# Attention with a gated feed-forward: the order of the first group and the places of the weight signs

## The chip, the cores and the metric

The kernel runs on one core of a Trainium2 chip. The metric is the device time of one execution in microseconds (us), as the median of five runs. The engines of a core are called here as the profile calls them: PE is TensorE (matrix products), PEld its weight load, DVE is VectorE, ACT is ScalarE, POOL is GpSimd and SP is SyncE, which here issues nearly all DMAs. L300 is line 300 of the kernel before; in the kernel after the change the same code stands 4 to 11 lines lower.

## The reference

The input x has 4 sequences of 512 positions and 1024 channels, in fp32.

```python
xn = layernorm(x)                                    # no scale, no shift
q, k, v = xn @ Wq, xn @ Wk, xn @ Wv                  # 16 heads of 64
q, k = rotary(q), rotary(k)
p = softmax(where(causal, q @ k.T, -1e9) / 8)        # per head, 512 x 512
s = (p @ v) @ Wo

r = softmax(xn @ gate_w.T)                           # router over 8 experts
g = silu((xn * (r @ in_scale)) @ sign(weight).T * (r @ out_scale) + bias)

out = x + s * g
```

## The kernel before

**Work.** Let b be one of the 4 sequences and g one of 4 groups of four heads. The kernel goes through 16 groups k = 0 to 15, in the order of (b, g). In each it projects the group's q, k and v (`project`, three matrices m = 0, 1, 2, so that one matrix is a key (b, g, m)), and on the way does the attention of group k − 1. After the last group come the rest of the feed-forward (`gated`, `ffn`) and the output projection (`project_out`), which the change does not touch.

**Start.** x arrives in four tiles of 128 rows. Each is normalised: two bn_stats of 512 columns, an aggregate (mean and variance), the root on ACT (`std`, L185), reciprocal and subtract-multiply on DVE (L193). PE then transposes it in eight 128 x 128 blocks (`transpose_x`, L205), four to a PSUM bank `xtp`, and ACT copies each bank into X (L211). X holds one sequence, channels by rows.

**Projection.** `project` multiplies a key's weights with X by a scheme of seven half-size products in place of eight. It needs four sums of weight quarters, S1 to S4 (`form_w`, DVE, L249), for every key, and four sums of X quarters, T1 to T4 (`form_x`, DVE, L261), once for a sequence. The order of the products before is: a11·b11 and a12·b21, which need neither S nor T; S3·T3; S2·T2; S1·T1; a22·T4; S4·b22. A product is four matmuls in the program and eight on the chip (fp32 takes two passes). While a key is worked on, DVE forms the S sums of the next. The results are put together by p1 and p5 copies on ACT (L333, L354), additions on DVE (L327, L356) and one on POOL (the part add, L355). The sums are called c for q and k and v for v. q and k then go through `rotary`: eight swaps on ACT for a pair of tiles (L269, L270), one operation on DVE (L271, `rot`), two on POOL (L272, L273).

**Attention.** `attention_pieces` lists the pieces for group k − 1: five transposes of probabilities (`ptp`, L457, copied to `pT`) for each of two pending units, `scores_1`, `scores_3` and `scores_02` with `values` between. A score block is: matmuls (L391), mask and row maximum on DVE (L402, L406), exponentials on ACT (L409), reciprocal on DVE (L417), scaling on POOL (L419). The probabilities from `scores_02` (p0) are transposed at the beginning of the next group.

**Extras.** In the groups with g = 0 (k = 0, 4, 8, 12) further pieces are put between these: `load_sign` and `make_sign` take two of the eight tiles of `weight` and make their signs (four DVE operations to a tile, L573 and L574), and `router` works in three steps: `lg` (64 matmuls, L495), its transpose `lt` with the softmax, and the transpose `rt` of the result. At k = 0 there are also `load_scales` (32 small DMAs on SP) and `split_scales`, once for in_scale and once for out_scale (isc, osc): one cast on ACT (L561) and three DVE operations over 128 x 1024 (L562 to L564).

**Order.** PE's instructions run in the order in which the program is written (a manual schedule). `interleave` writes them: after each piece come so many matmuls of the projection that 84 of them spread evenly over the pieces. DVE, ACT, POOL and SP get their order from a scheduler of the framework, except in a block at the start in which DVE and ACT follow the program too. The extras' places come from one rule:

```python
step = max(1, (len(pieces) + len(extra)) // (len(extra) + 1))
for n, e in enumerate(extra):
    pieces.insert(min(len(pieces), (n + 1) * step + n), e)
```

For k = 4, 8 and 12 this puts the six extras at places 3, 7, 11, 15, 19 and 21 of 0 to 21, in the order loads, router, sign, router, sign, router.

**Buffers.** All products, transposes and router results share a ring of four PSUM banks (`bank`); the scores have banks of their own. Three weight tiles of 1 MB are held. Later x tiles, the staged `weight` tiles and the scales share two buffers (`xip`). Every S and T sum has one buffer.

Of the kernel before, what the change touches and what calls it, by code (L numbers as in the profile page):

```python
# [22 lines left out]
NE = 8  # L23
# [28 lines left out]
def attn_gated_ffn_kernel(  # L52
# [111 lines left out]
    def load_x(b, t):  # L164
        if b == 0:
            xt = X1[:, t, :]
        else:
            xt = xip.tile([P, E], F32, tag="x", name=f"x_{b}_{t}")
        nc.sync.dma_start(out=xt, in_=x[(b * TPB + t) * P : (b * TPB + t + 1) * P, :])
        xin[b, t] = xt  # L170

    MV = {}

    def statistics(b, t):
        xt = xin[b, t]
        stats = st.tile([P, 2, 6], F32, tag="bn", name=f"bn_{b}_{t}")
        for j in range(2):

            tc.keep_in_program_order(
                nc.vector.bn_stats(stats[:, j, :], xt[:, j * HALF : (j + 1) * HALF])  # L180
            )
        mv = st.tile([P, 2], F32, tag="mv", name=f"mv_{b}_{t}")
        nc.vector.bn_aggr(mv, stats)
        std = st.tile([P, 1], F32, tag="std", name=f"std_{b}_{t}")
        nc.scalar.activation(std, mv[:, 1:2], AF.Sqrt, bias=eps)  # L185
        MV[b, t] = mv, std

# [5 lines left out]
        nc.vector.tensor_scalar(xt, xt, mv[:, 0:1], rstd, op0=ALU.subtract, op1=ALU.mult)  # L193

    def layernorm(b, t):
        statistics(b, t)
        normalize(b, t)

    def transpose_x(b, t, g):
        if b not in X:  # L200
            X[b] = xp.tile([P, NC, S], F32, tag="X", name=f"X_{b}")
        tp = tp_bank(f"xtp_{b}_{t}_{g}")
        for j in range(4):
            c = 4 * g + j
            nc.tensor.transpose(tp[:, j, :], xin[b, t][:, c * P : (c + 1) * P], ident)  # L205
        dst = X[b][:, 4 * g : 4 * g + 4, t * P : (t + 1) * P]

        if g == 0 and b > 0:
            nc.vector.tensor_copy(dst, tp)
        else:  # L210
            nc.scalar.copy(dst, tp)  # L211
        if g == 1:
            nc.sync.dma_start(
                out=xn_d[b, t].rearrange("p (c q) -> p c q", c=NC),
                in_=X[b][:, :, t * P : (t + 1) * P],
            )
# [62 lines left out]
    def project(b, g):  # L279

        for m in range(3):
# [15 lines left out]
            def product(ps, wq, xq):  # L297
                if m < 2:
                    for k in range(4):
                        nc.tensor.matmul(  # L300
                            ps, lhsT=wq[:, k, :], rhs=xq[:, k, :], start=(k == 0), stop=(k == 3)
                        )
                        yield
                else:

                    for j in range(2):
                        for k in range(4):
                            nc.tensor.matmul(  # L308
                                ps[:, j * P : (j + 1) * P],
                                lhsT=xq[:, k, j * P : (j + 1) * P],  # L310
                                rhs=wq[:, k, :],
                                start=(k == 0),
                                stop=(k == 3),
                            )
                            if k % 2:
                                yield

            def halves(n):

                ps = bank(f"pj_{un}_{n}")  # L320
                return ps, ps[:, :TH], ps[:, TH:]
# [14 lines left out]
                rotary(*turn.pop(0))  # L336
            _, p, r = halves(2)
            yield from product(r, SF[key, 3], TF[b, 3])
            yield from product(p, SF[key, 2], TF[b, 2])
            u2, u3 = part(2), part(3)  # L340
            add(u2, p, p1)
# [2 lines left out]
                rotary(*turn.pop(0))  # L344
            if after:
                form_w(after, 3)
            ps, p, r = halves(3)
            yield from product(r, SF[key, 1], TF[b, 1])
            if after:
                form_w(after, 1)  # L350
                form_w(after, 2)
# [300 lines left out]
            nc.scalar.copy(Z[q, i][:, k * HALF : (k + 1) * HALF], ps[n])  # L652


    for t in range(TPB):
        load_x(0, t)
    for m in range(3):
        load_w(0, 0, m)
    nc.sync.dma_start(out=cos_sb, in_=cos)
    nc.sync.dma_start(out=sin_sb, in_=sin)  # L660
    nc.sync.dma_start(out=gw[:, :, :NE], in_=gate_wT.rearrange("(c p) e -> p c e", p=P))

    first = project(0, 0)
    with tc.manual_schedule(engines={DVE, ACT}):
        statistics(0, 0)
        for t in range(TPB):
            if t + 1 < TPB:
                statistics(0, t + 1)
            if t == 2:
                next(first)  # L670
            normalize(0, t)
            for g in range(2):
                transpose_x(0, t, g)
            for _ in range((0, 3, 3, 0)[t]):
                next(first)
        for n in (3, 1, 2):
            form_w(keys[0], n)
        next(first)
        for n in (3, 1, 2, 4):
            form_x(0, n)  # L680
        form_w(keys[0], 4)

    def attention_pieces(k, late):
# [41 lines left out]
    for k, (b, g) in enumerate(groups):  # L725
        pieces = []
        if k > 0:
            pieces, late = attention_pieces(k - 1, late)
        extra = []
        if g == 0:  # L730
            extra = [
                lambda: (load_sign(2 * b), load_sign(2 * b + 1)),
                lambda: router(b, 0),
                lambda: make_sign(2 * b),
                lambda: router(b, 1),
                lambda: make_sign(2 * b + 1),
                lambda: router(b, 2),
            ]
            if b == 0:
                extra[5:5] = [lambda: (load_scales(in_scale), load_scales(out_scale))]  # L740
                extra += [lambda: split_scales(isc), lambda: split_scales(osc)]
        elif g == 1 and b + 1 < B:
            for t in range(2):
                load_x(b + 1, t)
        elif g > 1 and b + 1 < B:
            t0 = 2 * (g - 2)
            for t in range(t0, t0 + 2):
                layernorm(b + 1, t)
            extra = [
                lambda t=t, h=h: transpose_x(b + 1, t, h) for t in range(t0, t0 + 2) for h in range(2)  # L750
            ]
            if g == 2:
                extra.append(lambda: [load_x(b + 1, t) for t in (2, 3)])
# [4 lines that stand above are left out]
        if b == B - 1:  # L758

            if g < 2:  # L760
                load_xn(g)
            if g in (1, 2):
                pieces.insert(3, lambda: in_scales(g - 1, score_banks))
            if g == 3:
                z_place[0] = [xip.tile([P, E], F32, tag="x", name=f"z0_{i}") for i in range(2)]
                pieces.insert(3, lambda: out_scales(0, score_banks))
        fill = project(b, g) if k else first
        interleave(pieces, fill, 3 * 7 * 4)
        if g == NGRP - 1 and b + 1 < B:
            for n in (3, 1, 2, 4):  # L770
                form_x(b + 1, n)
# [297 lines left out]
```

## Time and profile before

| | |
|---|---|
| five runs | 1203.81, 1201.61, 1203.27, 1201.52, 1203.18 us |
| median | 1203.18 us |
| profiled execution | 1203.81 us, of which the span is 1202.1 us |
| mean granted TensorE clock | 0.995 |
| PE busy | 1172.8 us, 98% of the span |
| DVE busy | 774.6 us, 64% |
| ACT busy | 493.1 us, 41% |
| POOL busy | 536.3 us, 45% |
| DMA | 122.04 MB, 102 GB/s over the span |

The span runs from the first to the last instruction that the profiler recorded; the device time is 1.7 us longer. A timeline row gives start, busy time, engine, line, operation, tiles and shapes, and how many instructions it stands for; in brackets is the idle time of the engine before it, and what ended it. In a list of waits the three numbers are the sum in us, the number of waits and the longest.

### The profile page before, as it was taken

How to read it: one execution, taken by the hardware profiler on the slowest of the kernel's cores; microseconds unless marked ns; L12 is line 12 of the kernel's file. 1: busy time of each engine (PE TensorE's matmuls, PEld its weight loads, DVE VectorE, ACT ScalarE, POOL GpSimd, SP SyncE). 2: the span in 40 equal slices, each digit the busy share in tenths (PEclk: the TensorE clock that was granted, in tenths of full speed). 3: DMA queues.
4: the chain of work that ended last, by engine and by line, in shares of the span. 5: the costliest groups of instructions: out<-in, count | busy, mean ns of one | idle time of the engine just before them, and what ended most of it. 6: DMA issues, size and time to landing. Idle time of an engine off the chain costs nothing.

```text
span 1202.1 us, 17805 instructions
## 1 busy us (share of the span) xinstructions
PE 1172.8 (98%) x6696; PEld 890.5 (74%) x6696; DVE 774.6 (64%) x1395; ACT 493.1 (41%) x1134; POOL 536.3 (45%) x596
## 2 busy tenths in 40 slices
PE   6999999999999999999999999999999999999997
PEld 5988888878878887887888878887764456645663
DVE  6878676786767678576767866666864533453342
ACT  2453655344464644355464534446432121222120
POOL 0464536353443635243353534255355445544543
PEclk9999999999999999999999999999999999999999
DMA  8423423322143232223335122210503623432320
GB/s 298 127 70 119 135 80 95 117 86 93 44 126 112 80 118 94 64 80 114 105 98 184 52 74 80 76 52 18 202 14 135 194 81 106 145 109 71 106 70 35
DMA packets 59814, 122.04 MB, mean 102 GB/s; under 512 B 5200, under 2 KB 40528, under 8 KB 53584
## 3 DMA queue, kind: packets, MB, share of 16 engines
q1 hardware_dynamic: 55008, 111.98, 28.8%
q0 software_dynamic: 4720, 8.92, 2.1%
q8 instruction: 53, 0.87, 0.3%
q14 instruction: 33, 0.27, 0.1%
HBM read 95.45 MB, written 25.43 MB: 101 GB/s over the span
## 4 chain that ended last, share of the span: by engine, by line
PE 90%; DVE 7%; ACT 2%; issue 1%; POOL 0%; DMA 0%; ACTq 0%; DVEq 0%
PE pj L300 32%; PE wo L933 16%; PE pj L308 13%; PE ff L821 9%; PE pv L473 6%; PE sc L391 6%; PE ptp L457 6%; DVE nmx L406 2%; ACT p L409 1%; PE xtp L205 1%; DVE sc L402 1%; PE lg L495 1%; DVE rot L271 1%; DVE S L249 0%; DVE lo L633 0%
## 5 line engine op out<-in xcount | busy, mean ns | idle before, releaser
L419 POOL TENSOR_SCALAR p<-p,rs 128x128 f32<-128x128 f32 (+3 forms) x256 | 169.3, 673 | 204.6 <-DVE rs L417 204.6
L409 ACT ACTIVATE p<-sc,nmx 128x128 f32<-128x128 f32 (+3 forms) x256 | 132.7, 524 | 154.2 <-DVE nmx L406 145.8
L300 PE MATMUL pj<-T,S 128*128 128x256 f32 x768 | 182.3, 380 | 2.2 <-DVE T L261 2.2
L300 PEld LDWEIGHTS pj<-T,S 128*128 128x128 f32 x768 | 140.1, 190 | 20.6 <-DVE T L261 3.0
L300 PE MATMUL pj<-X,w 128*128 128x256 f32 x512 | 127.3, 391 | 6.4 <-DVE v L356 6.4
L355 POOL TENSOR_TENSOR part<-part,part 128x256 f32<-128x256 f32 x48 | 37.6, 783 | 200.4 <-ACT part L354 196.4
L272 POOL TENSOR_TENSOR sw<-sw,sin_sb 128x512 f32<-128x512 f32 x64 | 84.0, 1313 | 85.2 <-ACT sw L270 81.8
L300 PEld LDWEIGHTS pj<-X,w 128*128 128x128 f32 x512 | 95.5, 196 | 19.6 <-DVE v L356 7.1
L406 DVE TENSOR_REDUCE nmx<-sc 128x2 f32<-128x512 f32 (+3 forms) x128 | 103.6, 819 | 2.5
L249 DVE TENSOR_TENSOR S<-w 128x512 f32<-128x512 f32 x96 | 82.4, 860 | 32.8 <-PE pj L300 28.5
L821 PE MATMUL ff<-sg,hi 128*128 128x512 f32 x256 | 103.5, 404 | 0.0
L463 ACT COPY pT<-ptp 128x512 f32<-128x512 f32 x96 | 56.1, 587 | 115.2 <-PE ptp L457 114.3
L821 PE MATMUL ff<-sg,lo 128*128 128x512 f32 x256 | 99.9, 390 | 0.0
L457 PE MATMUL ptp<-ident,p 128*128 128x128 f32 x640 | 95.6, 273 | 2.9 <-DVE z_t L831 1.1
L308 PE MATMUL pj<-S,T 128*128 128x128 f32 x768 | 93.8, 280 | 2.3 <-DVE S L249 2.3
L308 PEld LDWEIGHTS pj<-S,T 128*128 128x128 f32 x768 | 89.7, 195 | 4.2 <-DVE S L249 2.5
L457 PEld LDWEIGHTS ptp<-ident,p 128*128 128x128 f32 x640 | 78.9, 141 | 18.5 <-DVE z_t L831 1.6
L269 ACT ACTIVATE sw<-c 32x512 f32<-32x512 f32 x128 | 80.4, 628 | 27.6 <-DVE c L327 25.7
L273 POOL TENSOR_TENSOR rot<-rot,sw 128x512 f32<-128x512 f32 x64 | 84.6, 1322 | 4.8
L391 PE MATMUL sc<-rot,rot 64*128 64x384 f32 (+3 forms) x512 | 82.0, 449 | 0.0
L270 ACT ACTIVATE sw<-c 32x512 f32<-32x512 f32 x128 | 80.4, 628 | 1.8
L473 PE MATMUL pv<-pT,v 128*64 128x256 f32 (+3 forms) x512 | 76.0, 439 | 0.0
(137 smaller groups left out, 1991.6 us busy)
## 6 DMA issues: line engine op xcount, KB each, us to landing
w<-in_wqkv SPq DMA_DIRECT2D x48, 1024.0 KB
x<-in_x SPq DMA_DIRECT2D x16, 512.0 KB
xn_d<-X SPq DMA_DIRECT2D x16, 512.0 KB
at_d<-at SPq DMA_DIRECT2D x32, 256.0 KB
xp<-xn_d SPq DMA_DIRECT2D x16, 512.0 KB
ap<-at_d SPq DMA_DIRECT2D x16, 512.0 KB
xr<-in_x SPq DMA_DIRECT2D x16, 512.0 KB
wb<-in_wb SPq DMA_DIRECT2D x8, 512.0 KB
```

What stands on the lines that cost most here:

```text
L272: nc.gpsimd.tensor_tensor(sw, sw, sin_sb, op=ALU.mult)
L273: nc.gpsimd.tensor_tensor(rot, rot, sw, op=ALU.add)
L300: nc.tensor.matmul(ps, lhsT=wq[:, k, :], rhs=xq[:, k, :], start=(k == 0), stop=(k == 3))
L308: nc.tensor.matmul(ps[:, j * P : (j + 1) * P], lhsT=xq[:, k, j * P : (j + 1) * P], rhs=wq[:, k, :], start=(k == 0), stop=(k == 3),)
L391: nc.tensor.matmul(ps[:, h, :], lhsT=Q[u][r : r + D, i * P : (i + 1) * P], rhs=K[u][r : r + D, : (i + 1) * P], start=True, stop=True,)
L406: nc.vector.tensor_reduce(nmx, ps, AX.X, ALU.max, negate=True)
L409: nc.scalar.activation(pt[:, h, :], ps[:, h, :], AF.Exp, bias=nmx[:, h : h + 1], accum_out=ssum[:, h : h + 1],)
L419: nc.gpsimd.tensor_scalar(pt[:, h, :], pt[:, h, :], rs[:, h : h + 1], 1.0, op0=ALU.mult, op1=ALU.mult,)
L457: nc.tensor.transpose(tp[:, k, :], probs(u, i)[:, h, j * P : (j + 1) * P], ident)
L473: nc.tensor.matmul(pv[r : r + D, j * P :], lhsT=V[u][:, j, r : r + D], rhs=PT[u][:, n, o : o + (TPB - j) * P], start=(j == 0), stop=(j == ...
L821: nc.tensor.matmul(acc, lhsT=part[q][:, i, c, :], rhs=sg[4 * k + c // 2][:, (c % 2) * HALF : (c % 2 + 1) * HALF], start=(c == 0 and part i ...
L933: nc.tensor.matmul(ps, lhsT=lhs[:, k, :], rhs=rhs[:, k, :], start=(k == 0), stop=(k == 3))
```

## The change

The change has five parts.

1. Before the input arrives PE does 26 transposes of the identity into a spare bank, whose results nobody reads.
2. The DMAs at the start are issued in another order: x tiles 0 and 1, the first half (512 KB) of the first key's weights, x tiles 2 and 3, the second half, the router's weights, then the other two keys' weights and the rotary tables.
3. In the block at the start the statistics of tile t + 1 are split: its first half stands ahead of the normalisation of tile t, its second half, the aggregate and the root behind the transposes and copies of tile t. The last copy of tile 3 goes to DVE. T and S sums are formed in the order T3, S1, T1, T2, S2, T4, S4. S3 is formed ahead of the normalisation of tile 3. In the very first key the product S1·T1 comes ahead of S2·T2.
4. For k = 0 the extras stand in a written list: router step 0 first, loads, router step 1, both signs, the scales' loads, router step 2, both splits, and two empty pieces.
5. For k = 4, 8 and 12 the extras stand at written places 0, 5, 8, 9, 12 and 15, in the order loads, sign, router, sign, router, router. With that `scores_02` moves from place 17 to 19.

In the order that results, PE's instructions differ from before only in the first two groups and in groups 4, 8 and 12. On the scheduled engines the following moves too: in group 1, DVE has the three osc operations of `split_scales` ahead of the four S sums of key (0, 1, 1), where before they stood ahead of those of (0, 1, 2); ACT has the osc cast behind the eight rotary swaps of (0, 1, 0); POOL has the part add of (0, 1, 0) behind the scaling of both p3 tiles; SP issues the weights of key (0, 1, 1) behind the 32 small DMAs of the scales.

```diff
--- before.py
+++ after.py
@@ -169,16 +169,18 @@
         nc.sync.dma_start(out=xt, in_=x[(b * TPB + t) * P : (b * TPB + t + 1) * P, :])
         xin[b, t] = xt
 
-    MV = {}
-
-    def statistics(b, t):
-        xt = xin[b, t]
-        stats = st.tile([P, 2, 6], F32, tag="bn", name=f"bn_{b}_{t}")
-        for j in range(2):
-
-            tc.keep_in_program_order(
-                nc.vector.bn_stats(stats[:, j, :], xt[:, j * HALF : (j + 1) * HALF])
-            )
+    BN, MV = {}, {}
+
+    def half_statistics(b, t, j):
+        if j == 0:
+            BN[b, t] = st.tile([P, 2, 6], F32, tag="bn", name=f"bn_{b}_{t}")
+
+        tc.keep_in_program_order(
+            nc.vector.bn_stats(BN[b, t][:, j, :], xin[b, t][:, j * HALF : (j + 1) * HALF])
+        )
+
+    def deviation(b, t):
+        stats = BN[b, t]
         mv = st.tile([P, 2], F32, tag="mv", name=f"mv_{b}_{t}")
         nc.vector.bn_aggr(mv, stats)
         std = st.tile([P, 1], F32, tag="std", name=f"std_{b}_{t}")
@@ -193,7 +195,9 @@
         nc.vector.tensor_scalar(xt, xt, mv[:, 0:1], rstd, op0=ALU.subtract, op1=ALU.mult)
 
     def layernorm(b, t):
-        statistics(b, t)
+        half_statistics(b, t, 0)
+        half_statistics(b, t, 1)
+        deviation(b, t)
         normalize(b, t)
 
     def transpose_x(b, t, g):
@@ -205,7 +209,7 @@
             nc.tensor.transpose(tp[:, j, :], xin[b, t][:, c * P : (c + 1) * P], ident)
         dst = X[b][:, 4 * g : 4 * g + 4, t * P : (t + 1) * P]
 
-        if g == 0 and b > 0:
+        if (g == 0 and b > 0) or (g == 1 and (b, t) == (0, TPB - 1)):
             nc.vector.tensor_copy(dst, tp)
         else:
             nc.scalar.copy(dst, tp)
@@ -336,6 +340,10 @@
                 rotary(*turn.pop(0))
             _, p, r = halves(2)
             yield from product(r, SF[key, 3], TF[b, 3])
+            if pos == 0:
+
+                bank3 = halves(3)
+                yield from product(bank3[2], SF[key, 1], TF[b, 1])
             yield from product(p, SF[key, 2], TF[b, 2])
             u2, u3 = part(2), part(3)
             add(u2, p, p1)
@@ -344,8 +352,11 @@
                 rotary(*turn.pop(0))
             if after:
                 form_w(after, 3)
-            ps, p, r = halves(3)
-            yield from product(r, SF[key, 1], TF[b, 1])
+            if pos:
+                ps, p, r = halves(3)
+                yield from product(r, SF[key, 1], TF[b, 1])
+            else:
+                ps, p, r = bank3
             if after:
                 form_w(after, 1)
                 form_w(after, 2)
@@ -652,32 +663,55 @@
             nc.scalar.copy(Z[q, i][:, k * HALF : (k + 1) * HALF], ps[n])
 
 
-    for t in range(TPB):
-        load_x(0, t)
-    for m in range(3):
+
+    idle = bank("idle")[:, :P]
+    for _ in range(26):
+        nc.tensor.transpose(idle, ident, ident)
+    load_x(0, 0)
+    load_x(0, 1)
+
+    W[0, 0, 0] = wp.tile([P, 2, NC, P], F32, tag="w", name="w_0_0_0")
+
+    def load_half_w(i):
+        nc.sync.dma_start(
+            out=W[0, 0, 0][:, i].rearrange("p c n -> p (c n)"), in_=wqkv[0, 0][:, i * E : (i + 1) * E]
+        )
+
+    load_half_w(0)
+    load_x(0, 2)
+    load_x(0, 3)
+    load_half_w(1)
+    nc.sync.dma_start(out=gw[:, :, :NE], in_=gate_wT.rearrange("(c p) e -> p c e", p=P))
+    for m in (1, 2):
         load_w(0, 0, m)
     nc.sync.dma_start(out=cos_sb, in_=cos)
     nc.sync.dma_start(out=sin_sb, in_=sin)
-    nc.sync.dma_start(out=gw[:, :, :NE], in_=gate_wT.rearrange("(c p) e -> p c e", p=P))
 
     first = project(0, 0)
     with tc.manual_schedule(engines={DVE, ACT}):
-        statistics(0, 0)
+        half_statistics(0, 0, 0)
+        half_statistics(0, 0, 1)
+        deviation(0, 0)
         for t in range(TPB):
             if t + 1 < TPB:
-                statistics(0, t + 1)
-            if t == 2:
-                next(first)
+                half_statistics(0, t + 1, 0)
+            else:
+                form_w(keys[0], 3)
             normalize(0, t)
             for g in range(2):
                 transpose_x(0, t, g)
-            for _ in range((0, 3, 3, 0)[t]):
+            if t + 1 < TPB:
+                half_statistics(0, t + 1, 1)
+                deviation(0, t + 1)
+            for _ in range((0, 5, 2, 0)[t]):
                 next(first)
-        for n in (3, 1, 2):
-            form_w(keys[0], n)
         next(first)
-        for n in (3, 1, 2, 4):
-            form_x(0, n)
+        form_x(0, 3)
+        form_w(keys[0], 1)
+        form_x(0, 1)
+        form_x(0, 2)
+        form_w(keys[0], 2)
+        form_x(0, 4)
         form_w(keys[0], 4)
 
     def attention_pieces(k, late):
@@ -728,17 +762,33 @@
             pieces, late = attention_pieces(k - 1, late)
         extra = []
         if g == 0:
-            extra = [
-                lambda: (load_sign(2 * b), load_sign(2 * b + 1)),
-                lambda: router(b, 0),
-                lambda: make_sign(2 * b),
-                lambda: router(b, 1),
-                lambda: make_sign(2 * b + 1),
-                lambda: router(b, 2),
-            ]
-            if b == 0:
-                extra[5:5] = [lambda: (load_scales(in_scale), load_scales(out_scale))]
-                extra += [lambda: split_scales(isc), lambda: split_scales(osc)]
+            loads = lambda: (load_sign(2 * b), load_sign(2 * b + 1))
+            signs = [lambda n=n: make_sign(2 * b + n) for n in range(2)]
+            routing = [lambda n=n: router(b, n) for n in range(3)]
+            if k == 0:
+                pieces = [
+                    routing[0],
+                    loads,
+                    routing[1],
+                    *signs,
+                    lambda: (load_scales(in_scale), load_scales(out_scale)),
+                    routing[2],
+                    lambda: split_scales(isc),
+                    lambda: split_scales(osc),
+                    lambda: None,
+                    lambda: None,
+                ]
+            else:
+
+                for at, piece in (
+                    (0, loads),
+                    (5, signs[0]),
+                    (8, routing[0]),
+                    (9, signs[1]),
+                    (12, routing[1]),
+                    (15, routing[2]),
+                ):
+                    pieces.insert(at, piece)
         elif g == 1 and b + 1 < B:
             for t in range(2):
                 load_x(b + 1, t)
```

## The prediction, made before the changed kernel ran

> **What bounds the kernel now.** I read the page first (busy shares, the chain that ended last), then what TensorE waited for, then the timeline around each wait.
>
> ```profile
> PE 1172.8 (98%) x6696; PEld 890.5 (74%) x6696; DVE 774.6 (64%) x1395; ACT 493.1 (41%) x1134; POOL 536.3 (45%) x596
> PE 90%; DVE 7%; ACT 2%; issue 1%; POOL 0%; DMA 0%; ACTq 0%; DVEq 0%
> ```
>
> TensorE (PE) is the bound: busy 98%, 90% of the chain. Only its idle time and its slow time can be won; no matmul of the network is removed. Where it idled:
>
> ```profile
> PE xtp L205 <- DVE x L193: 9.0, 2, 8.8
> PE pj L300 <- DVE v L356: 6.4, 3, 2.2
> PE pj L308 <- DVE S L249: 2.3, 1, 2.3
> PE pj L300 <- DVE T L261: 2.2, 2, 1.6
> ```
>
> So: 8.8 us before the first transpose, three waits of 2.19, 2.195 and 2.03 us (6.42 together) where groups 5, 9 and 13 begin, one of 2.35 us at 93 us, and 1.55 + 0.61 us for the T forms at the start. The change touches the code around every one.
>
> Idle time costs twice. After the wait at 93.09 us the 128-column matmuls start 0.213 us apart instead of 0.112, until 96.8:
>
> ```profile
> 93.10:96.80 3.70, 3.70 (x18) 3.70 (x19) 3.67 (x4) 2.25 (x4) 3.70 (x7) 0.54 0.92 312
> ```
>
> (columns: window, length, busy PE, PEld, DVE, ACT, POOL, then the granted clock, 0.54.) The same happens for 3.41 us after the waits at 479 and 694 us, not after the one at 265.9. All slow stretches end and begin on one grid of 3.41 us; a window that was 31 to 40% busy was followed by a slow one, a window 46% busy was not (the 265.9 wait is split over two). A slow window loses half: 1.71 us. At the start the cadence is the slow one until 14.89; the window 8.06–11.47, 71% busy, did not end it, the next, fully busy, did.
>
> **The change, part 1: the start.** Before:
>
> ```profile
> 8.76 1.94 PE L205 MATMUL xtp<-ident,x 128*128 128x128 f32 x8 [8.76 <-DVE x L193]
> ...
> 11.21 0.30 ACT L185 ACTIVATE std<-mv,eps 128x1 f32<-128x1 f32 x1
> 12.13 0.59 ACT L211 COPY X<-xtp 128x512 f32<-128x512 f32 x1 [0.61 <-PE xtp L205]
> ...
> 20.82 1.99 PE L300 MATMUL pj<-T,S 128*128 128x256 f32 x8 [1.55 <-DVE T L261]
> ```
>
> The 26 idle transposes run from about 1.5 us (ident is written at 1.48); 26 x 0.213 (the slow cadence of L205) = 5.5 us, to 7.1. They lie in the 8.76 us in which PE had nothing, and cost nothing. Tile 0 is normalised 0.79 us earlier (half of tile 1's statistics, 0.64, and the 0.21 aggregate now stand behind it): ends 7.81. From 7.1 until the first product PE has only the first transposes, so a clock raised by the dummies would meet a window under 40% busy and fall again. I take it as slow there.
>
> What the reader must see in the ACT rows is the order: std of tile 2 (11.21) ran ahead of the copies of tile 1 (12.13). In the changed order std of tile t+1 stands behind both copies of tile t, so the tiles form a chain: norm end, +0.15, transposes and two copies 2.56 at slow clock, std 0.29, reciprocal and norm 1.05 = 4.05 us. Tile 1 ends at 11.9 (before 10.92). Five quarter products (10 matmuls) now stand in PE between the transposes of tiles 1 and 2, so tile 2's transposes wait for them: they start at 16.4 if the clock rises at 14.9, at 17.9 if at 18.3. X is complete at 21.3 or 23.0; I take R = 22.0 (before 18.43 + 1.07 = 19.5), 20.3 if PE were fast throughout. The last copy on VectorE in parallel saves 0.5 and is in this. After X: before, 13.0 us to the end of the first key (32.51), made of the T3 wait, five products of 1.73, the 0.61 wait, the router's lg of 1.95 and its transpose. After, lg stands where PE waited for T3: 1.95 + 5 x 1.73 + 0.11 = 10.7. End 32.7, **+0.2 us** (−1.5 with R = 20.3, +1.2 with 23.0). The loads move past each other on SP's queue, but x3 landed by 9.1 and the first w by 11.6 against norms at 16 and 20: hidden. Signs of tiles 0 and 1 now fall into the second key: 2.1 us each, beside about 8 us of other DVE work in its 12.1 us of PE: hidden.
>
> The skill's page "TensorE: Matmul & The Clock Gate", Part 4, says that PE-mode transposes do not count as busy for the clock gate, which speaks against the dummies altogether: by that rule R = 20.3 is out, and the sum stays as I have it. The rows leave it open, since the window of transposes that left the clock slow was only 71% busy; by them R = 20.3 can happen, and the sum would be 1.7 lower.
>
> **Part 2: a new wait in key (0,1,1).** Before, and the wait that it replaces:
>
> ```profile
> 86.39 1.06 ACT L561 CAST osc<-scales 128x1024 fp32r<-128x1024 f32 x1
> ...
> 91.13 1.30 DVE L564 SCALAR_TENSOR_TENSOR osc<-osc,is_high,scales 128x1024 fp32r<-128x1024 f32 x1
> ...
> 92.35 1.37 DVE L249 TENSOR_TENSOR S<-w 128x512 f32<-128x512 f32 x2
> 93.09 4.05 PEld L308 LDWEIGHTS pj<-S,T 128*128 128x128 f32 x21 [2.54 <-DVE S L249]
> 93.09 4.13 PE L308 MATMUL pj<-S,T 128*128 128x128 f32 x20 [2.35 <-DVE S L249]
> ```
>
> split_scales(osc) stood in DVE's queue ahead of the S forms of (0,1,2), and PE waited 2.35. In the changed order it is a key earlier: DVE has the two rot0 operations, then L562 to L564 for osc, then all four S forms of (0,1,1); and ACT has the osc cast behind the eight rotary swaps of (0,1,0). On SP, w of (0,1,1) is issued behind the 32 small scale loads; it still lands some 20 us ahead of use. On the clock of before: PE ends (0,1,0) at 72.79 and has two products without S, until 76.24. POOL's part add (L355), which c and so the swaps wait for, now stands behind the scaling of p3: p3 73.0 to 74.33, add to 75.07, c 75.1 to 75.5. Eight swaps x 0.64 end at 80.7; cast 1.05, 81.75; L562, L563, L564 to 84.95; S3 0.65, 85.6. PE loses 85.66 − 76.24 = **9.4 us** (8.2 if the part add could run ahead of p3 and c came at 73.9; 10.3 with the longest POOL rows, 1.13 for the add and 1.2 for a scaling). Such a gap fills two windows, so one to two slow windows follow: 1.7 to 3.4, I take 2.25. The old wait and its slow window go: 2.35 + 1.71 = 4.06. Sum 9.4 + 2.25 − 4.06 = **+7.6**.
>
> **Part 3: signs of groups 4, 8 and 12.** What made the 2.19 us:
>
> ```profile
> 262.89 0.71 DVE L573 TENSOR_SCALAR sg<-wb 128x512 fp32r<-128x512 f32 x1
> ...
> 263.53 0.41 DVE L406 TENSOR_REDUCE nmx<-sc 128x2 f32<-128x256 f32 x1
> 263.85 0.73 DVE L574 SCALAR_TENSOR_TENSOR sg<-wb,sg 128x512 fp32r<-128x512 f32 x1
> 264.03 0.37 ACT L409 ACTIVATE p<-sc,nmx 128x128 f32<-128x128 f32 x1 [1.95 <-DVE nmx L406]
> ...
> 264.73 0.37 ACT L354 COPY part<-pj 128x256 f32<-128x256 f32 x1
> ...
> 265.19 0.66 DVE L356 TENSOR_TENSOR v<-pj,part 128x512 f32<-128x512 f32 x1
> 265.90 2.86 PE L300 MATMUL pj<-X,w 128*128 128x256 f32 x12 [2.19 <-DVE v L356]
> ```
>
> Signs sit between DVE's mask and max operations; the last block's exponentials on ACT come late, the p5 copy (L354) behind them, v behind that, and PE needs the PSUM bank that v frees. After, all signs are earlier in the group, p5 is ahead of those exponentials, and the router's rt transpose takes its ring bank earlier, so the next group's first product gets a bank long free. Gain 6.42 and the two slow windows at 479 and 694, 3.41. What is late next: scores_02 moves two pieces nearer to the next group's first ptp transpose, which needs p0 from POOL (L419). PE reaches it after scores of 1.93 and 22 matmuls of 0.223, 6.85 us after scores_02 starts (before 8.3 to 10.6); from scores to p0 takes 6.44 to 6.99 in the groups without signs, 8.72 to 8.89 with them. So 0 to 0.15 a group: 0.3 in all. Sum −6.42 + 0.3 − 3.41 = **−9.5**.
>
> The same page ("Why this matters for your kernels") allows idle gaps up to about 3 us before the clock falls. The rows differ: it fell after 2.35, 2.195 and 2.03 us, and they decide. By the page part 3 would bring the waits alone, and the sum would be 3.4 higher.
>
> **Sum.** 1203.81 (the profiled execution, span 1202.1 and 1.7 around it) + 0.2 + 7.6 − 9.5 = **1202.1**. That execution is 0.63 above the median of 1203.18; the five differ by about one slow window. A measurement of this kernel tells 0.2% (2.4 us: below 1200.8, above 1205.6) from no change, so my forecast is no measurable change, two large terms that cancel.
>
> **Rivals.** R1, faster: the dummies leave PE fast. R = 20.3 gives 1.7 less, 1200.4; with c early (8.2) 1199.2, with one slow window only 1198.6. For it: the dummies fill more than one window; against: nothing to hold the clock from 7.1 to 12. R2, slower: the waits of part 3 return as ptp waits for POOL. It decides from a chain of about 8.1 us (1.2 x 3 − 0.3 = 3.3 more, 1205.4); at the longest row, 8.89, it is 3 x 2.04 − 0.3 + 3.4 of slow windows = +9.2, 1211. Against: the 8.7 to 8.9 rows are those with signs between. R3: the start is not advanced at all (R = 23.0), the new wait is 10.3 and two slow windows follow: 1.0 + 0.9 + 1.15 more, 1205.2.
>
> **How the numbers follow.** Base 0.40 (its own range 1200.8 to 1205), R1 0.33, R2 0.15, R3 0.12. Half of R3 is taken as slower, since two more unseen waits of 0.2 us put it there. Faster 0.33, same 0.40 + 0.06 = 0.46, slower 0.15 + 0.06 = 0.21. Low: R1's 1198.6 less 0.6 (profiled run to median), 1198.0; high: R3 with the 1.8 by which R2's chain at 7.5 us exceeds mine (3 x 0.65 − 0.15), 1207.0. R2's far end stays out.
>
> **What would show it.** Right: one PE wait of 8 to 10 us at L304 for S (L253) near 76 us; no wait of L304 for v (L367) at groups 5, 9, 13; no 2.3 us wait at 93; granted clock still low near 10 us; X complete near 22 us. Wrong: the long wait missing or under 5 us (then about 1195), waits of 1 us and more at L468 for p (L430) near 264, 477 and 691, or the first key ending before 31.

## The result and the profile after

The changed kernel takes 1203.70 us (median of 25 runs, 1202.20 to 1204.76) against 1202.81 us before (45 runs, 1199.65 to 1204.07). The ratio is 1.0009, with an interval of 1.0004 to 1.0015: about one microsecond slower. That lies inside the 0.2% that the prediction called no change, and inside its range, but on the other side of zero: for the profiled execution 1.7 us less than before was forecast, and 0.9 us more came. With so many runs a difference smaller than 0.2% can be told from zero. The profiled execution took 1204.71 us, its span 1203.0 us.

What PE waited for in the changed kernel (sum in us, number of waits, the longest):

```profile
PE pj L304 <- DVE S L253: 10.4, 1, 10.4
PE xtp L209 <- DVE x L195: 3.9, 3, 2.0
PE ptp L468 <- POOL p L430: 2.3, 5, 0.6
```

The three waits for v (6.4 us together) and the one of 2.3 us for S are gone. In their place stands one long wait for S, three of 0.50 us for p (the other 0.8 of that row was there before) and, spread over the start, 3.9 us of waits for normalised tiles (9.0 before).

The two traces can be laid beside each other at places where PE begins the same key. The offset is after minus before; a step is what the stage in between added.

| PE begins | before | after | offset | step | forecast |
|---|---|---|---|---|---|
| key (0,0,1) | 32.51 | 32.54 | +0.03 | +0.03 | +0.2 |
| key (0,0,2) | 44.71 | 45.25 | +0.54 | +0.51 | 0 |
| key (0,1,0) | 58.48 | 59.02 | +0.53 | 0 | 0 |
| group 2 | 104.19 | 113.47 | +9.28 | +8.75 | +7.6 |
| second key of group 13 | 709.69 | 710.55 | +0.86 | −8.42 | −9.5 |
| end of the span | 1202.1 | 1203.0 | +0.9 | 0 | 0 |

The start and the two large terms went the way that the prediction said. The two were each about 1.1 us worse than forecast, and the second key, (0,0,1), which it held for free, cost 0.5 (the row of (0,0,2)).

**The long wait.** The timeline of the changed kernel, from the sum c on which the rotary swaps wait, to the product that waits for S:

```profile
75.71 0.42 DVE L331 TENSOR_TENSOR c<-pj,part 128x256 f32<-128x256 f32 x1 [1.38 <-POOL part L366]
...
81.30 1.04 ACT L572 CAST osc<-scales 128x1024 fp32r<-128x1024 f32 x1
...
82.38 1.33 DVE L573 TENSOR_TENSOR scales<-scales,osc 128x1024 f32<-128x1024 f32 x1 [4.92 <-ACT osc L572]
82.71 2.12 POOL L277 TENSOR_TENSOR rot<-rot,sw 128x512 f32<-128x512 f32 x1
83.75 1.64 DVE L574 TENSOR_SCALAR scales<-scales,is_high 128x1024 f32<-128x1024 f32 x1
...
85.42 1.28 DVE L575 SCALAR_TENSOR_TENSOR osc<-osc,is_high,scales 128x1024 fp32r<-128x1024 f32 x1
86.62 1.29 DVE L253 TENSOR_TENSOR S<-w 128x512 f32<-128x512 f32 x2
...
87.36 5.16 PE L304 MATMUL pj<-T,S 128*128 128x256 f32 x12 [10.42 <-DVE S L253]
```

The order is the forecast one, and up to the cast so are the times, once the 0.53 us by which the key begins later are added: the forecast then has c at 75.63 (75.71 came) and the cast at 81.23 (81.30 came). From there 1.0 us is lost: L574 took 1.64 us where its rows had been 0.77 and 0.83 before and 0.75 earlier in this trace, and L573 1.33 instead of 1.22. DVE idled 4.92 us ahead of L573, with the S sums queued behind it; SP had issued their weights at 50.32.

**The clock.** Windows of the changed kernel (length, busy time of PE, PEld, DVE, ACT and POOL, granted clock, DMA share, GB/s):

```profile
6.73:10.13 3.40, 1.46 (x11) 0.99 (x9) 2.76 (x8) 1.27 (x3) 0.00 (x0) 1.00 1.01 402
10.14:16.96 6.82, 6.01 (x18) 4.95 (x19) 4.47 (x9) 1.37 (x3) 0.00 (x0) 0.50 1.04 398
81.82:92.06 10.24, 4.70 (x11) 3.81 (x12) 7.87 (x9) 0.80 (x2) 7.34 (x10) 0.50 0.50 155
```

The idle transposes raised the clock at 6.72. The next window was 43% busy (1.46 of 3.40), and the clock fell for two windows. Behind the long wait PE worked from 87.36 to 92.06 at half clock, a loss of 2.35 us (2.25 was taken).

**The start.**

```profile
1.53 5.57 PE L669 MATMUL idle<-ident 128*128 128x128 f32 x26 [1.53 <-POOL ident masks.py:199]
7.89 1.09 PE L209 MATMUL xtp<-ident,x 128*128 128x128 f32 x8 [0.78 <-DVE x L195]
10.95 1.97 PE L209 MATMUL xtp<-ident,x 128*128 128x128 f32 x8 [1.97 <-DVE x L195]
...
20.16 1.06 PE L209 MATMUL xtp<-ident,x 128*128 128x128 f32 x8 [1.19 <-DVE x L195]
```

The first eight transposes run at full clock (1.09 us), the next eight at half (1.97). Each of the xtp rows waits for x, the chain that was forecast. The last copy into X ended at 21.95; 22.0 was worked out. In the other five profiled executions with this start it ended between 20.4 and 22.2, with the clock: 20.4 to 21.2 where one window was slow (four executions), 22.2 where two were, as here.

### The profile page after: what moved, and what is told of

The parts are those of the page before. It is cut to its first block, busy times and chain, and to the rows that moved or that the text cites. A ratio compares the mean times of both kernels' runs of the same rounds, so it can differ in the third digit from the quotient of the medians.

```text
span 1203.0 us, 17849 instructions
## 1 busy us (share of the span) xinstructions
PE 1175.9 (98%) x6722; PEld 893.6 (74%) x6722; DVE 760.7 (63%) x1396; ACT 492.0 (41%) x1133; POOL 532.9 (44%) x596
## 4 chain that ended last, share of the span: by engine, by line
PE 92%; DVE 5%; ACT 1%; DMA 1%; issue 1%; POOL 0%; SPq 0%; ACTq 0%; DVEq 0%
PE pj L304 31%; PE wo L983 16%; PE pj L312 15%; PE ff L871 9%; PE pv L484 6%; PE sc L402 6%; PE ptp L468 6%; PE xtp L209 1%; DVE nmx L417 1%; ACT p L420 1%; PE lg L506 1%; DMA x<-in_x 1%; DVE S L253 0%; DVE sc L413 0%; DVE lo L644 0%
## 5 line engine op out<-in xcount | busy, mean ns | idle before, releaser
L430 POOL TENSOR_SCALAR p<-p,rs 128x128 f32<-128x128 f32 (+3 forms) x256 | 166.8, 664 | 189.7 <-DVE rs L428 189.7
L304 PE MATMUL pj<-T,S 128*128 128x256 f32 x768 | 185.2, 384 | 10.4 <-DVE S L253 10.4
L304 PE MATMUL pj<-X,w 128*128 128x256 f32 x512 | 124.6, 386 | 0.0
L304 PEld LDWEIGHTS pj<-X,w 128*128 128x128 f32 x512 | 94.3, 193 | 12.6 <-issue 1.4
L468 PEld LDWEIGHTS ptp<-ident,p 128*128 128x128 f32 x640 | 78.5, 141 | 20.4 <-POOL p L430 3.5
L277 POOL TENSOR_TENSOR rot<-rot,sw 128x512 f32<-128x512 f32 x64 | 84.2, 1316 | 4.8
```

The source lines that it names most:

```text
L277: nc.gpsimd.tensor_tensor(rot, rot, sw, op=ALU.add)
L304: nc.tensor.matmul(ps, lhsT=wq[:, k, :], rhs=xq[:, k, :], start=(k == 0), stop=(k == 3))
L430: nc.gpsimd.tensor_scalar(pt[:, h, :], pt[:, h, :], rs[:, h : h + 1], 1.0, op0=ALU.mult, op1=ALU.mult,)
L468: nc.tensor.transpose(tp[:, k, :], probs(u, i)[:, h, j * P : (j + 1) * P], ident)
```

## The experiments

A time is always read beside runs of the kernel before on the same chip. Where a difference to the changed kernel is given, it is the difference of the two ratios to before, times 1202.8. One thing is needed to read the traces: the grid of 3.41 us on which the clock is set lies differently in each execution. The same code of the start had one slow window in four profiled executions, whose first key ended between 31.01 and 31.79, and two in two, where it ended at 32.54 and 32.77. So a single trace is good for 1.7 us at the start and no better.

### Part 5 alone

```diff
+            else:
+                loads, r0, s0, r1, s1, r2 = extra
+                extra = []
+                for at, piece in ((0, loads), (5, s0), (8, r0), (9, s1), (12, r1), (15, r2)):
+                    pieces.insert(at, piece)
```

> The kernel before with part 5 of the change alone (written places of the extras in groups 4, 8 and 12). Theory: the parts add up, and part 5 is worth what the offset between the two traces says, 9.28 - 0.86 = 8.4 us: 1202.8 - 8.4 = 1194.4, with no wait for v at groups 5, 9 and 13, no slow clock there, and three waits of about 0.5 us for p from POOL. Rival: the gain in the changed kernel was partly a recovery from the long wait of 10.4 us (other engines ran ahead in it); then part 5 alone brings clearly less, under 6 us, and the waits for p are longer than 0.5 us.

Measured: ratio 0.9942 (0.9926 to 0.9957), about 7 us less than before (5.2 to 8.9). In the trace the offset to the kernel before goes from −2.71 at group 2 to −11.14 at the second key of group 13: −8.43, as the −8.42 in the changed kernel. The three waits for p were 0.50, 0.50 and 0.50 us. By the trace the rival falls: the part is worth the same without the long wait ahead of it. The times alone would not exclude its 6 us. The medians show less than the trace. The 8.43 includes the two slow windows of before at 479 and 694 us (3.41), and the spread of the runs of before suggests that not every execution has them.

### Both splits early

```diff
-        for t in range(P // NE):
-            nc.sync.dma_start(out=v[NE * t : NE * (t + 1), :], in_=src)
+        nc.sync.dma_start(out=v, in_=src[None, :, :].to_broadcast((P // NE, NE, E)))
```

> The changed kernel with one DMA for each scale table (a source read 16 times over) in place of 16, so that the scheduler sees the scales arrive early and puts both splits ahead of the S sums of group 1. Theory: the wait of 10.42 us and the 2.2 us of slow clock behind it are the whole cost of part 4; both go, and no other comes: 1203.7 - 12.6 = 1191.1. Rival: the 6.4 us of split work on DVE make another wait where they now stand (key (0,0,2)), of 2 us or more, with a slow window: above 1194.

Measured: 1196.43 us, ratio 0.9958 (0.9944 to 0.9973), 6.1 us less than the changed kernel and not 12.6. The long wait is gone, and two others came. One is of 2.76 us, where PE waits for rot with the first scores: on DVE the isc split stood ahead of both rotary operations of (0,0,1), and two osc operations between them. The other, of 1.20 us, is at 69.12, for exponentials on ACT, and not for rot. The rival's wait and time hold; the slow window that it added did not follow in the profiled execution.

### The scales' loads one piece later

```diff
+                    routing[2],
                     lambda: (load_scales(in_scale), load_scales(out_scale)),
-                    routing[2],
```

> The changed kernel with the loads of the scales one piece later, behind the load of the weights of key (0,1,1) on SP. Nothing else is moved by hand. Theory: it is the place of that load in the scheduler's plan that put the S sums of (0,1,1) behind split_scales(osc) on DVE; with it back, the wait at (0,1,1) goes, and a wait of about 7 us comes at (0,1,2), where the osc cast now stands behind six swaps on ACT and the S sum behind two of the three osc operations: 1203.7 - 3.4 = 1200.3. Rival: the order of the loads has nothing to do with it, the wait at (0,1,1) stays near 10 us and the time at 1203.7.

Measured: ratio 1.0004 (0.9993 to 1.0015), 0.6 us less than the changed kernel, within the uncertainty. The wait at (0,1,1) went and one of 8.88 us came at (0,1,2). So the two swapped lines decide what DVE's order is, as the theory says. That they do it through which load stands first on SP in the scheduler's plan is its reading; the run shows the swap and the new order. The size was off: L574 again ran beside POOL's rotary operations, two of them, and took 1.73 us, and the S sum behind it 1.75 instead of 0.69.

### Without the idle transposes

```diff
-    idle = bank("idle")[:, :P]
-    for _ in range(26):
-        nc.tensor.transpose(idle, ident, ident)
```

> The changed kernel without the 26 transposes of the identity. Theory: they raise the clock for the first eight transposes only (start to start 0.11 us in place of 0.21) and it has fallen again by the second tile; without them the first tile's copies come about 0.85 us later, and tile 2's transposes wait for PE anyway: 0 to 0.9 us more, 1203.7 to 1204.6, with the first eight transposes taking 1.94 us and the clock up again near 15 us. Rival: the clock counts on from the idle transposes, and without them the start stays at half clock one window longer: 1.7 us more, 1205.4.

Measured: ratio 1.0025 (1.0015 to 1.0035), 1.9 us more than the changed kernel, with intervals that touch. The first eight transposes took 1.94 us, and the clock rose at 15.93. In this trace the first key ended at 32.47, as in the executions with the idle transposes and two slow windows (32.54 and 32.77), and 0.7 to 1.5 us later than in those with one. The medians lie nearer to the rival, but the intervals allow nothing as well as 3.7 us; how much the idle transposes are worth, and where in the start, stays open here.

### The operation beside POOL in another form

```diff
-        nc.vector.tensor_scalar(v, v, is_high[:, 1:2], None, op0=ALU.mult)
+        nc.vector.tensor_tensor(v, v, is_high[:, 1:2].to_broadcast((P, E)), op=ALU.mult)
```

> The changed kernel with the middle operation of split_scales (a tensor_scalar of 128 x 1024) as a tensor_tensor against the broadcast column. In the changed kernel that operation took 1.64 us beside a POOL operation (itself 2.12 instead of 1.26), where it takes 0.75 to 0.83 without one. Theory: the two engines hold each other up when DVE runs a tensor_scalar; as tensor_tensor it takes about 1.2 us with or without POOL, the POOL operation beside it 1.3, and the long wait is 10.4 - 0.4 = 10.0 us. Rival: DVE and POOL slow each other whatever the form; then it takes over 1.6 us again, POOL's 2 us, and the wait is 10.4 or more.

One profiled run (1202.43 us):

```profile
81.79 2.12 POOL L277 TENSOR_TENSOR rot<-rot,sw 128x512 f32<-128x512 f32 x1
82.83 2.17 DVE L574 TENSOR_TENSOR scales<-scales,is_high 128x1024 f32<-128x1024 f32 x1
```

The theory falls: the tensor_tensor took 1.22 us alone (for isc, at 65.08) and 2.17 beside L277. The two forms are held up by about the same, 0.9 us. POOL's 2.12 came again, but says little on the form: L277 had begun beside the subtraction ahead of L574 (81.46 to 82.79), which is the same in both versions. The wait of 10.09 us says nothing on this, since the scheduler put the S sum ahead of the last osc operation in this version.

### One more piece behind scores_02

```diff
                     pieces.insert(at, piece)
+                pieces.append(lambda: None)
```

> The changed kernel with one empty piece more at the end of groups 4, 8 and 12, so that scores_02 lies 4 of 23 pieces from the end instead of 3 of 22. Theory: the three waits of 0.5 us for p are only a matter of distance (7.12 us from scores_02 to the first ptp transpose, 7.62 needed); with 14.6 instead of 11.5 steps of the projection between (0.45 us each) PE comes after 8.5 us and the waits go: 1203.7 - 1.5 = 1202.2. Rival: bringing the pieces before it closer together makes waits for the other transposes, and nothing is gained.

Measured: ratio 0.9993 (0.9985 to 1.0002), 1.9 us less than the changed kernel. The three waits for p are gone and no other came. The cause was the distance, as the theory says.

### The root ahead of the copies

```diff
             normalize(0, t)
-            for g in range(2):
-                transpose_x(0, t, g)
             if t + 1 < TPB:
                 half_statistics(0, t + 1, 1)
                 deviation(0, t + 1)
+            for g in range(2):
+                transpose_x(0, t, g)
```

> The changed kernel with the second half of tile t + 1's statistics, its aggregate and its root ahead of the transposes and copies of tile t, as before the change. Theory: the 1.19 us for which PE waits ahead of tile 3's transposes is the price of the chain root - norm - transposes - copies - root; without it X is complete about 1.2 us earlier and the first key ends about 1.2 us earlier where the clock is the same: 1203.7 - 1.2 = 1202.5. Rival: the products between the tiles and the clock set X, the wait only moves, and the first key ends when it did.

Measured: ratio 1.0003 (0.9994 to 1.0012), 0.7 us less than the changed kernel, in the direction of the theory but not beyond the uncertainty. In the trace the wait of 1.19 us is gone, and the first key ends at 30.22, against 31.01 to 31.79 in the four profiled executions with the changed start and also one slow window: 0.8 to 1.6 us. The nearest in the place of that window (12.41 to 15.83, here 12.18 to 15.60) is the one of 31.79.

### osc in group 1

The scales' DMAs are joined as above, and out_scale goes to group 1:

```diff
-                    lambda: (load_scales(in_scale), load_scales(out_scale)),
+                    lambda: load_scales(in_scale),
...
-                    lambda: split_scales(osc),
+                    lambda: None,
...
-            for t in range(2):
-                load_x(b + 1, t)
+            load_x(b + 1, 0)
+            if b == 0:
+                pieces.insert(1, lambda: (load_scales(out_scale), split_scales(osc), load_x(1, 1)))
+            else:
+                load_x(b + 1, 1)
```

> The changed kernel with one DMA for each scale table, and out_scale's load and split taken from group 0 into group 1, so that DVE's order has the three osc operations behind the rotary of (0,0,1) and S3 of (0,1,0), and ahead of the S sums of (0,1,1). Theory: the long wait with its slow clock (12.6 us together) goes, and the waits of 2.76 and 1.20 us for rot that the experiment with both splits in group 0 showed do not come, since rot no longer stands behind osc: 1203.7 - 12.6 = 1191.1. Rival: 3.2 us of DVE work cannot be put anywhere in groups 0 and 1 without a wait of a similar size: 1194 or more.

Measured: 1193.47 us, ratio 0.9923 (0.991 to 0.9935), 10.3 us less than the changed kernel. The long wait is gone. One wait for rot of 1.49 us remained, with a slow window behind it (60.20 to 63.61): 1.49 + 1.71 = 3.2 us in the profiled execution, where the median is 2.4 us above the theory. The median lies between the theory's 1191.1 and the rival's 1194.

### The start as it was

The kernel before with the written lists of parts 4 and 5, and nothing of parts 1 to 3.

> The changed kernel without parts 1 to 3 (no idle transposes, loads, statistics, sums and products of the start as before); the written lists of parts 4 and 5 stay, so lg stands right behind X here too. Theory: what the start of the change won it won by putting lg where PE waited for T3, which this kernel keeps; the rest lost (X complete at 21.95 against 19.5). X comes at 19.5, and the first key ends near 30.5 to 31 instead of 32.5: 1203.7 - 1.7 = 1202.0, with the wait of 10.4 us unchanged. Rival: the idle transposes and the early tile 0 are worth something by themselves; then the first key ends at 32.5 or later and the time is 1204 or more.

Measured: 1201.39 us, ratio 0.999 (0.9981 to 0.9999): 2.3 us less than the changed kernel, with the wait of 10.4 us unchanged. PE around lg:

```profile
18.33 1.96 PE L495 MATMUL lg<-X,gw 128*32 128x128 f32 x64
20.22 1.99 PE L300 MATMUL pj<-T,S 128*128 128x256 f32 x8
22.56 1.78 PE L300 MATMUL pj<-T,S 128*128 128x256 f32 x7 [0.35 <-DVE T L261]
```

lg fills the time in which PE had waited 1.55 us for T3, and nothing of parts 1 to 3 is needed for it. The first key ended at 29.68. So parts 1 to 3 cost about 2 us (0.6 to 4.1 by the ends of the two intervals); what the start of the change won, part 4's list won.

### The edits together

The version with osc in group 1, the further piece and the root ahead of the copies:

> The three edits that helped put together on the changed kernel: one DMA for each scale table with osc in group 1, one empty piece more in groups 4, 8 and 12, and the root of tile t + 1 ahead of the copies of tile t. Theory: they lie in different stages and add up: 1193.5 - 2.1 - 0.6 = 1190.8, with one wait of about 1.5 us for rot near 58 us. Rival: they overlap, 1192.5 or more.

Measured: 1188.95 us, ratio 0.9885 (0.987 to 0.99). They add up, and somewhat more (1190.8 expected). The wait for rot is there with 1.50 us, but no slow window followed it in the profiled execution. Then the middle operation of the split on ACT:

```diff
-        nc.vector.tensor_scalar(v, v, is_high[:, 1:2], None, op0=ALU.mult)
+        nc.scalar.activation(v, v, AF.Copy, scale=is_high[:, 1:2])
```

> As the version with the three edits, and the middle operation of split_scales (times is_high) goes from DVE to ACT as an activation with a scale column. Theory: the wait of 1.5 us for rot comes from osc operations on DVE running beside the rotary operations on POOL, each slowed; with 0.75 to 1.75 us less on DVE the wait shrinks to under 0.8 us and its slow clock goes: 1.5 to 2.5 us less than without the edit. Rival: the first osc operation alone (1.75 us beside POOL) makes the wait, and it stays at 1.5 us.

Measured: 1192.55 us, ratio 0.9912 (0.9899 to 0.9926): slower by 3 us. The theory falls, and the rival too: the wait for rot grew to 2.98 us. ACT has the new operation for isc ahead of the rotary swaps. POOL's second pair of rotary operations began 25.31 us behind the end of the first key (57.25), against 24.06 in the version without it (54.10): 1.25 later. The other 1.9 us between the two traces stood there when the first key ended (31.94 and 30.04), with two slow windows and one; that part belongs to the clock's grid and not to the edit. In place of that, with DVE's operation back, 14 idle transposes more behind tile 0:

```diff
+            if t == 0:
+                for _ in range(14):
+                    nc.tensor.transpose(idle, ident, ident)
```

> As the version with the three edits, and 14 more transposes of the identity behind the transposes of tile 0, where PE waits 1.65 us for tile 1 and the granted clock falls. Theory: transposes count as work for the clock; 14 x 0.11 = 1.5 us keep the stretch from 8 to 12 us busy, the slow window near 10 to 15 us goes, and the first key ends 1.3 to 1.7 us earlier: about 1.5 us less than without them. Rival: transposes do not count, the clock falls as before, and the 14, at half clock 3 us, hold the transposes of tile 1 up by 1 us or more.

Measured: 1187.97 us, ratio 0.9875 (0.9861 to 0.9888), 15 us less than before. The start on PE:

```profile
7.74 1.09 PE L209 MATMUL xtp<-ident,x 128*128 128x128 f32 x8 [1.24 <-DVE x L195]
8.67 1.69 PE L707 MATMUL idle<-ident 128*128 128x128 f32 x14
11.28 1.09 PE L209 MATMUL xtp<-ident,x 128*128 128x128 f32 x8 [0.92 <-DVE x L195]
12.93 2.43 PE L304 MATMUL pj<-X,w 128*128 128x256 f32 x10 [0.55 <-ACT X L215]
```

From tile 0 on everything runs at full clock: 1.09 us for eight transposes of tile 1, 2.43 for ten products that took 4.50 in the changed kernel. The clock records show no slow window from 5.49 us to the last few of the span. The theory's mechanism holds, at two thirds of its size: the median is 1.0 us lower than without them, where about 1.5 was expected (the first key ended at 29.28 instead of 30.04), and the four runs (1187.77 to 1188.08) all lie below the four without them (1188.29 to 1190.26). This is the fastest version of the study.

## Why the prediction was right and wrong

**What bounds the kernel.** Right: all of the difference lies in PE's waits and its half clock.

**Part 1, the start (+0.2).** R, the time at which X is complete, was 21.95 for 22.0, the offset +0.03. The chain from root to root, the products between tiles 1 and 2, and the fall of the clock after the idle transposes all stand in the trace. That R was hit so closely is partly luck: the same start gave 20.4 to 22.2 in six executions. The pair settles no more than 1.7 us; the start as it was, with lg early, is the firmer test. The term had netted a gain of 2.3 from lg's place (13.0 us after X against 10.7) with a loss of 2.5 from the later X. The two are separate: the first belongs to part 4, and parts 1 to 3 by themselves cost about 2 us.

The rule that transposes do not count for the clock, which was weighed there, is contradicted here: 26 transposes raised the clock at 6.72, and 14 more kept it up.

**The signs in the second key ("hidden").** Wrong by 0.5 us. Where key (0,0,2) begins, PE waited 0.35 us for a PSUM bank, which a part addition on DVE (L331) frees, and that stood behind a sign operation of 0.67 us:

```profile
44.19 0.67 DVE L585 SCALAR_TENSOR_TENSOR sg<-wb,sg 128x512 fp32r<-128x512 f32 x1
...
44.78 0.41 DVE L331 TENSOR_TENSOR part<-pj,part 128x256 f32<-128x256 f32 x1
...
45.25 1.49 PE L312 MATMUL pj<-w,X 128*128 128x128 f32 x11 [0.35 <-DVE part L331]
```

Counting DVE's total work in the key (8 of 12.1 us) did not see a queue of a moment.

**Part 2 (+7.6, came 8.75).** The mechanism, the order and the place were right; the term was mis-sized by 1.0 us in the wait (9.4, came 10.42). The failing step is "L562, L563, L564 to 84.95". The rows of before for the middle operation, L563, have 0.23 us of POOL arithmetic beside them (0.77 us at 66.07) or none (0.83):

```profile
87.60 1.22 DVE L562 TENSOR_TENSOR scales<-scales,osc 128x1024 f32<-128x1024 f32 x1
87.64 1.76 POOL L355 TENSOR_TENSOR part<-part,part 128x256 f32<-128x256 f32 x1
...
89.78 0.83 DVE L563 TENSOR_SCALAR scales<-scales,is_high 128x1024 f32<-128x1024 f32 x1
```

POOL's rotary operations follow the swaps that the step counted, and run just then: L277 was under way when the middle operation began, and it took 1.64 us. The two rows above it show the same from the other side: L562 began 0.04 us ahead of the part add and kept its 1.22, and the part add took 1.76 where 0.73 was read for it at 265.18. The upper bound of 10.3 stretched POOL's own rows, and left DVE's as they were; the wait of 10.42 lay above it, and above the 8 to 10 us that the prediction named as its sign.

**Part 3 (−9.5, came −8.42).** The waits and the two slow windows went as forecast. The step that failed is "0 to 0.15 a group": the waits for p are 0.50 each. In group 4 of the changed kernel:

```profile
269.82 0.98 DVE L253 TENSOR_TENSOR S<-w 128x512 f32<-128x512 f32 x1
...
270.72 1.28 DVE L417 TENSOR_REDUCE nmx<-sc 128x2 f32<-128x256 f32 x2
...
272.27 1.08 POOL L430 TENSOR_SCALAR p<-p,rs 128x128 f32<-128x128 f32 x2 [1.02 <-DVE rs L428]
...
273.06 0.66 PE L468 MATMUL ptp<-ident,p 128*128 128x128 f32 x4 [0.50 <-POOL p L430]
```

Scores begin at 265.44, so p came after 7.62 us, where 6.44 to 6.99 had been read in groups without signs; PE was there after 7.12 instead of 6.85. An S sum of 0.98 us stands between mask and maximum here; in group 5 it is an addition of 0.41 (L331, at 319.93). That this makes the difference is read from the order and was not tried; that the distance decides was. Rival R2 had the mechanism, and its chain of 8.1 us was not reached.

**The sum.** With 0.51 for the second key, 1.15 more in part 2, 1.08 more in part 3 and 0.17 less in part 1, 1202.1 becomes 1204.7, which the profiled execution took. The two large terms cancelled as forecast, and what tipped the sign were three steps of 0.5 to 1.2 us. A forecast whose result is the rest of such a subtraction has no sign of its own, and the chances (faster 0.33 above slower 0.21) gave it one.

## What to carry to other kernels

Written places in a program move only what follows the program: here the order of two lines, and of the loads behind them, decided through a scheduler's plan where a vector engine stood idle for 4.9 us. When a step is costed that is put beside another engine's step, take durations from rows in which that engine ran too, and look which of the two began first. And a short wait on the matrix engine that can't be removed may be worth filling with idle transposes: here 14 of them, in a wait of 2.2 us, saved 1.0 us.

## What was not expected of the hardware

**DVE and POOL take turns.** L574 alone takes 0.75 us, L277 alone 1.26. Side by side, L277 took 2.12 and L574 1.64: nearly what one waits for the other. L277 began at 82.71, while the subtraction L573 was running on DVE, and ended 1.12 us after it (83.71); L574 began at 83.75, while L277 was running, and ended 0.56 us after that (84.83). In the version with osc in group 1 the 128 x 1024 subtraction of the two splits took 1.74 and 1.76 us beside POOL instead of 1.22. The Trainium skill, "SBUF — State Buffer", section "Who interferes with whom", says that a DVE operation with two SBUF inputs contends with a GpSimd operation that reads SBUF, and its section "SBUF: two separate sides" that whichever starts first holds the shared ports for its whole instruction, also against a DVE operation in a two-port mode. The 2.17 us of the tensor_tensor, which has two inputs, agrees with that. The 1.64 of the tensor_scalar does if it ran in such a mode, which no row here says.

**The clock's grid is not tied to the kernel.** It rose at 14.89, 12.61 and 13.19 us in three profiled executions of the same old start. The Trainium skill, "TensorE: Matmul & The Clock Gate", section "What's actually happening", says that the window runs freely; the traces agree. That the spread of the kernel's times comes from this is not shown: the four runs of the version without a slow window lie within 0.31 us, but the four of the version with the multiplication on ACT, which had two slow windows in its profile, also lie within 0.63.

**The busy share of a window does not decide alone.** The prediction read that windows 31 to 40% busy were followed by a slow one and a window 46% busy was not, and 43% in the changed kernel fits. But a window 56% busy (1.92 of 3.41 us, with the wait of 1.49 us in it) was followed by a slow one in the version with osc in group 1 (56.79 to 60.20), and one just as busy (with a wait of 1.50) was not in the version with the three edits (55.57 to 58.98). What tells the two apart stays open.
